# One more head transposed by VectorE in a two-layer masked attention kernel on one core: what the time does

## The chip, the core and the metric

The kernel runs on one core of a Trainium2 chip. The core has TensorE (PE in the profile; PEld is its weight load, which overlaps the matmuls), VectorE (DVE), ScalarE (ACT), GpSimd (POOL), SyncE (SP, which here only issues transfers) and 16 DMA engines that serve every transfer queue. The metric is device time in microseconds, the median of several executions.

## The reference

Two layers over 16 graphs of 1024 nodes with 256 features. Each normalises its input, clips it at zero, attends over the graph's adjacency matrix and adds the result to the input.

```
# layer 0: 8 heads of 32, masked by adj
h = maximum(layernorm(x), 0)
Q, K, V = heads of (h @ Wq.T + bq), (h @ Wk.T + bk), (h @ Wv.T + bv)
scores  = einsum('bhnd,bhmd->bhnm', Q, K) * 32 ** -0.5
attn    = softmax(where(adj == 0, -inf, scores))
x = x + (concatenated heads of attn @ V) @ Wo.T + bo
# layer 1: a score by kind of edge, with leaky relu
h = maximum(layernorm(x), 0)
e_k    = leaky_relu(einsum('bid,bjd->bij', h * a_k[:, 0], h), 0.2)     # k = 0..3
scores = where(adj == k + 1, e_k, -9e15)
x = x + softmax(scores) @ h
```

The adjacency holds 0 and 1 only, so the main path of layer 1 needs e_0 alone; a second path for other kinds stands behind a test at the end and does not run.

## The kernel before

A tile is 128 rows of one graph; a graph has NT = 8 tiles, the batch 128. One pass of the outer loop is called a slot here: slot s works on tile t = s mod 8 of graph s // 8 (`now`). Each slot has eight steps, h = 0 to 7, one for each head. The order of the instructions on every engine is the order in which this loop writes them (a manual schedule): nothing overtakes on an engine or on a queue. So a slot holds, interleaved by hand: layer 0 of tile s (`now`), the end of layer 0 of tile s-1 (`was`), the norm of tile s-2 (`gone`), layer 1 of tile s-9 (`edge`) and the end of layer 1 of tile s-10 (`edge_was`), and the projections of a tile that is wanted nine slots later (`piece`, `piece_was`). In the first nine slots there is no layer 1 yet; after the last slot a loop by itself ends the remaining tiles of layer 1 (the tail).

A head's way through layer 0:

- `scores(h)` (line 460): two matmuls of 512 columns into one of two PSUM places, `sides`. Heads 4 and 6 take the second, all others the first; layer 1's scores use the second too.
- `softmax_max(h)` (472): VectorE scales and masks the scores into an SBUF buffer p (ring of 4) and leaves the row extremum.
- `softmax_exp(h)` (489): ScalarE takes the exponential, one step later.
- The probabilities must be transposed. `turn` (589, 590) does it with eight 128x128 TensorE transposes into PSUM and two copies to SBUF. `turn_blocks` and `place_blocks` (381, 386) do it with one VectorE transpose inside 32x32 blocks into a buffer of the ring `blocks`, and four SyncE transfers of 128 KB that move the blocks to their places in a buffer pT (ring of 7). Which heads go which way is in `BY_BLOCKS` and `MIXED`: in tiles 1 to 6 heads 0, 1, 4, 5 by VectorE, in tile 0 heads 4, 5, in tile 7 heads 0, 1. Heads 6 and 7 always go by TensorE. It happens two steps after the scores: head 6 and head 7 of a tile in steps 0 and 1 of the next slot.
- A head whose rows are wanted in another order than the block transpose leaves them has its exponential written in permuted order into a second p buffer (`softmax_exp`, the branch on `MIXED`).
- `combine(0)` (525), 64 small matmuls in step 7, multiplies heads 0 to 3 by V; `combine(1)` does heads 4 to 7 in step 3 of the next slot. Its matmuls go round the heads: the first is of head 4, the second of head 5, the third of head 6, the fourth of head 7, and so on.

Of layer 1: `score` (625, 631), `softmax_max` (654), `bend` (663, a relu by ScalarE into its own buffer `less`), `leak` (672 to 674, GpSimd), `softmax_exp` (678), then `turn_blocks` and `place_blocks` in step 0 of the next slot, `gather` (696) in steps 5 and 6, `store` (703, 705) in step 6. `gather` sums into `sums_place`, which `combine` uses too.

SyncE's queue takes, in the order of the slot: layer 1's four pieces (step 0), head 0's four (step 2), head 1's four and the next queries (step 3), the output of layer 1 and head 4's four (step 6), the kept rows x1d (551, step 6), head 5's four (step 7), and in tiles 7 and 0 eight loads of keys between them.

The steps around the change, in the order of the code:

```
now.scores(h)
now.softmax_max(h)
ending.softmax_exp(eh)              # the head before
if h == 3: was.combine(1); piece_was.biased(); was.combined()
if turning and th in by_blocks(turning.t):
    turning.turn_blocks(th); turning.place_blocks(th)      # th = h - 2, of `was` in steps 0 and 1
if h == 0: edge.score(0); gone.normed(); edge_was.turn_blocks(); edge_was.place_blocks()
```

Of the kernel before, what the change touches and what calls it, by code (L numbers as in the profile page):

```python
# [8 lines left out]
F32 = mybir.dt.float32  # L9
# [5 lines left out]
ALU = mybir.AluOpType  # L15
AX = mybir.AxisListType

P = 128
HEADS = 8
HD = 32  # L20
# [4 lines left out]
NEG_INF = -9000000000000000.0  # L25
MASKED = -1e30
MIXED = (0, 1, 4, 5)
BY_BLOCKS = {7: (0, 1), 0: (4, 5)}


def by_blocks(t):
    return BY_BLOCKS.get(t, MIXED)

# [6 lines left out]
FLOOR = 1e28  # L40
# [7 lines left out]
def gnn_kernel(  # L48
# [35 lines left out]
    work = ctx.enter_context(tc.tile_pool(name="work", bufs=2))  # L84
# [103 lines left out]
    class Piece:  # L188
# [5 lines left out]
        def __init__(self, b, first, n=1):  # L194
            self.b, self.first, self.n = b, first, n
            self.cols = slice(first * P, (first + n) * P)
            self.projected, self.halved, self.queries = [], [], []
            self.tags = ("xin", "h0", "hT", "halves", "hTm") if n == 1 else ("pT", "pT", "pT", "p", "blocks")

        def buffer(self, i, shape, dtype=F32):  # L200
            tag = self.tags[i]
            if tag == "pT":
                return ptp.tile(shape, dtype, tag=tag, name=tag)
            bufs = {"p": 4, "blocks": 3, "halves": 2 if self.n == 1 else 4, "qt": 2, "xin": 2}.get(tag, 1)
            return work.tile(shape, dtype, tag=tag, name=tag, bufs=bufs)

        def load(self, queue=nc.gpsimd):
# [163 lines left out]
    def mixed(rows):  # L371

        return rows.rearrange("(b k) n -> k b n", b=NB)
# [3 lines left out]
        return rows.rearrange("(k b) n -> b k n", b=NB)  # L377

    def blocks_of(p):
        blocks = work.tile([P, NB, NT, HD], F32, tag="blocks", bufs=3)  # L380
        nc.vector.transpose(blocks.rearrange("p b j q -> p j b q"), p)  # L381
        return blocks.rearrange("p b j q -> p b (j q)")

# [8 lines left out]
    h1s, x1ds, masks = {}, {}, {}  # L392
# [22 lines left out]
    class Attend:  # L415
# [3 lines left out]
        def __init__(self, b, t):  # L419
            self.b, self.t = b, t  # L420
            self.rows = slice(t * P, (t + 1) * P)
            self.probs, self.turned = {}, {}

        def load_queries(self):
            self.qt = work.tile([P, HEADS, P], F32R, tag="qt")
            q = qds[self.b][self.t].rearrange("c (r d) u w n -> (d u w) (c r) n", d=HD)
            nc.sync.dma_start(out=self.qt.bitcast(F32), in_=q)
# [26 lines left out]
            )  # L454

        def scores(self, h):
            self.ps = sides[h in (4, 6)]
            for nh in range(N // HALF):
                cols = slice(nh * HALF, (nh + 1) * HALF)
                nc.tensor.matmul(  # L460
                    self.ps[:, cols],
                    lhsT=self.qt[:, h, :],
                    rhs=keysets[self.b][h][:, cols],
                    start=True,
                    stop=True,
                )

        def softmax_max(self, h):

            p = work.tile([P, N], F32, tag="p", bufs=4)  # L470
            nmx = small.tile([P, 1], F32, tag="nmx")
            nc.vector.tensor_tensor_reduce(  # L472
                out=p, in0=sides[h in (4, 6)], in1=self.neg, scale=-SCALE, scalar=FLOOR,
                op0=ALU.add, op1=ALU.min, accum_out=nmx,
            )
            self.probs[h] = (p, nmx)
# [20 lines left out]
        def turn_blocks(self, h):  # L497
            self.blocks = blocks_of(self.probs[h][0])
# [94 lines left out]
    class Edges:  # L593


        def __init__(self, b, t, last=False):
            self.b, self.t, self.last = b, t, last
            self.rows = slice(t * P, (t + 1) * P)
            self.side = sides[t % 2 if last else 1]
            self.tags = {"sel": ("p", 4), "pT1": ("pT", 7)} if last else {}  # L600
            if last and t % 2:
                self.tags |= {"ha": ("hT", 1), "x1b": ("x1", 1)}

        def buffer(self, tag, shape):
            tag, bufs = self.tags.get(tag, (tag, 1))
# [53 lines left out]
        def bend(self):  # L659

            if not self.last:
                self.less = work.tile([P, N], F32, tag="less", name="less", bufs=1)
                nc.scalar.activation(self.less, self.sel, AF.Relu, scale=1 - 1 / SLOPE)  # L663

        def leak(self):
# [20 lines left out]
        def turn_blocks(self):  # L686
            self.blocks = blocks_of(self.sel)
# [4 lines left out]
        def gather(self, half):  # L692

            for j in range(half * NT // 2, (half + 1) * NT // 2):
                for a in range(NB):
                    nc.tensor.matmul(  # L696
                        sums_place[a * HD : (a + 1) * HD, :], lhsT=self.pT[:, j, a], rhs=h1s[self.b][:, j, :],
                        start=(j == 0), stop=(j == NT - 1),
                    )

        def store(self):
            rec = small.tile([P, 1], F32, tag="rec1")
            nc.vector.reciprocal(rec, self.total)  # L703
            ot = work.tile([P, D], F32, tag="h0", bufs=1)
            nc.vector.scalar_tensor_tensor(ot, sums_place, rec, self.x1, ALU.mult, ALU.add)  # L705
            nc.sync.dma_start(out=mixed(out[self.b, self.rows, :]), in_=ot)


# [65 lines left out]
    def attend_of(s):  # L774
        return Attend(*divmod(s, NT)) if 0 <= s < B * NT else None
# [9 lines left out]
    with tc.manual_schedule():  # L785
        first = [Piece(0, 0, 4), Piece(0, 4, 4)]
        piece_was, piece_next = Piece(1, 0), piece_of(0)
        now, nxt = attend_of(0), attend_of(1)
# [39 lines left out]
        piece, edge, edge_was = piece_next, None, None  # L828
# [8 lines left out]
        for s in range(B * NT + 1):  # L837
            b, t = divmod(s, NT)
# [8 lines left out]
            for h in range(HEADS):  # L847
                ending, eh = (now, h - 1) if h >= 1 else (was, HEADS - 1)
                turning, th = (now, h - 2) if h >= 2 else (was, HEADS + h - 2)
# [38 lines left out]
                if h == 3:  # L888
                    if was:
                        was.combine(1)  # L890
                    if piece_was:
                        piece_was.biased()
                    if was:
                        was.combined()
                if turning and th in by_blocks(turning.t):
                    turning.turn_blocks(th)
                    turning.place_blocks(th)
                elif turning:
                    turning.turn(th, 0)
                    turning.turn(th, 1)  # L900


                if h == 0:
                    if edge:
                        edge.score(0)
                    if gone:
                        gone.normed()
                    if edge_was:
                        edge_was.turn_blocks()
                        edge_was.place_blocks()  # L910
                if h == 1:
                    if gone:
                        gone.turn_normed()
                    if piece_was:
                        piece_was.project(1, 0)
                        piece_was.project(1, 1)
                    if was:
                        was.reciprocals()
                    if piece_nxt:
                        piece_nxt.load()  # L920
                if h == 2:
# [54 lines left out]
            gone, was, now, nxt = was, now, nxt, nxt2  # L976
            edge_was, edge = edge, edge_nxt
# [85 lines left out]
```

## Time and profile before

| what | value |
|---|---|
| median of 3 runs | 3078.11 us (3077.22 to 3081.56) |
| the profiled execution's own time | 3080.43 us |
| its span in the trace | 3078.1 us |
| busy: PE, ACT, DVE, POOL | 2964.1, 2654.2, 2514.7, 2172.2 us |
| TensorE transposes of layer 0 (589) | 4608, busy 603.9 us |
| ScalarE copies of them (590) | 1024, mean 590 ns |
| VectorE block transposes of p (381) | 456, mean 1238 ns |
| transfers of block pieces (386) | 2304, median 3.4 us from issue to landing |
| granted TensorE clock, mean | 0.996 |

Busy time is the union of an engine's instructions. The mean of a TensorE matmul is longer than its share, because matmuls overlap: 4608 transposes of 274 ns each take 603.9 us together, 131 ns each. A wait is put down to the instruction or transfer that released it. The landing of a transfer is counted from its issue on the queue.

The profiled execution's time is 2.3 us over its span, for what lies around it, and 2.3 us over the median of the runs.

### The profile page before, as it was taken

How to read it: one execution, taken by the hardware profiler on the slowest of the kernel's cores; microseconds unless marked ns; L12 is line 12 of the kernel's file. 1: busy time of each engine (PE TensorE's matmuls, PEld its weight loads, DVE VectorE, ACT ScalarE, POOL GpSimd, SP SyncE). 2: the span in 40 equal slices, each digit the busy share in tenths (PEclk: the TensorE clock that was granted, in tenths of full speed). 3: DMA queues.
4: the chain of work that ended last, by engine and by line, in shares of the span. 5: the costliest groups of instructions: out<-in, count | busy, mean ns of one | idle time of the engine just before them, and what ended most of it. 6: DMA issues, size and time to landing. Idle time of an engine off the chain costs nothing. (4 is left out here: it accounts for less than half of the span.)

```text
span 3078.1 us, 96258 instructions
## 1 busy us (share of the span) xinstructions
PE 2964.1 (96%) x36722; PEld 2230.7 (72%) x36722; DVE 2514.7 (82%) x4453; ACT 2654.2 (86%) x5159; POOL 2172.2 (71%) x2999
## 2 busy tenths in 40 slices
PE   7889999999999999999999999999999999999997
PEld 4667777777777777777777777777777777776664
DVE  5878888888888888888888788888888888888884
ACT  5889888899888898889889888988989888898872
POOL 3657777777777777777777777777777777776542
PEclk9999999999999999999999999999999999999999
DMA  6776777878777786777777777787777777777653
GB/s 239 217 227 201 235 236 225 253 219 245 229 224 235 227 257 212 227 251 221 247 230 232 233 231 244 221 253 223 221 248 226 248 212 234 236 227 239 191 164 100
DMA packets 597828, 695.68 MB, mean 226 GB/s; under 512 B 63280, under 2 KB 528560, under 8 KB 597360
## 3 DMA queue, kind: packets, MB, share of 16 engines
q1 hardware_dynamic: 528288, 477.29, 52.0%
q0 software_dynamic: 66960, 210.04, 20.8%
q8 instruction: 295, 4.83, 0.7%
q10 hardware_dynamic: 2112, 2.10, 0.2%
q14 instruction: 173, 1.42, 0.1%
HBM read 252.98 MB, written 134.22 MB: 126 GB/s over the span
## 5 line engine op out<-in xcount | busy, mean ns | idle before, releaser
L472 DVE CUSTOM_DVE_ANT_0 p<-s,neg 128x1024 f32<-128x1024 f32 x1024 | 1235.6, 1207 | 220.8 <-PE s L460 189.5
L489 ACT ACTIVATE p<-p,nmx 128x1024 f32<-128x1024 f32 x1024 | 1249.6, 1224 | 135.5 <-DVE nmx L472 127.1
L460 PE MATMUL s<-k,qt 128*128 128x512 f32 x2048 | 759.3, 452 | 22.2 <-DVE nmx L472 13.8
L590 ACT COPY pT<-trp 128x512 f32<-128x512 f32 x1024 | 548.7, 590 | 92.8 <-PE trp L589 92.3
L589 PE MATMUL trp<-ident,p 128*128 128x128 f32 x4608 | 603.9, 274 | 3.6 <-ACT pT L590 1.5
L589 PEld LDWEIGHTS trp<-ident,p 128*128 128x128 f32 x4608 | 531.3, 140 | 101.7 <-DVE pT L590 9.6
L381 DVE STREAM_TRANSPOSE blocks<-p 128x1024 f32<-128x1024 f32 x456 | 564.4, 1238 | 12.7 <-ACT p L678 10.6
L525 PE MATMUL acc<-pT,v 128*32 128x128 f32 x16384 | 533.3, 275 | 36.9 <-ACT recT L519 24.9
L525 PEld LDWEIGHTS acc<-pT,v 128*32 128x32 f32 x16384 | 454.3, 110 | 146.3 <-ACT recT L519 79.9
L696 PE MATMUL acc<-h,pT 128*32 128x256 f32 x8192 | 493.0, 382 | 8.0 <-DVE ot L705 7.9
L440 POOL TENSOR_SCALAR neg<-adj 128x1024 bf16<-128x1024 int32 x128 | 467.7, 3654 | 43.7 <-ACT neg L452 34.4
L460 PEld LDWEIGHTS s<-k,qt 128*128 128x128 f32 x2048 | 322.0, 190 | 116.4 <-DVE nmx L472 43.7
L696 PEld LDWEIGHTS acc<-h,pT 128*32 128x32 f32 x8192 | 241.0, 109 | 210.3 <-issue 62.4
L674 POOL TENSOR_TENSOR sel<-sel,less 128x1024 f32<-128x1024 f32 x120 | 286.6, 2388 | 69.4 <-ACT less L663 48.1
L631 PE MATMUL s<-h1T,ha 128*128 128x512 f32 (+2 forms) x744 | 272.8, 490 | 2.6 <-ACT h1T L568 0.5
L672 POOL TENSOR_SCALAR less<-top 128x1 f32<-128x1 f32 x120 | 31.8, 265 | 272.9 <-DVE top L654 272.8
L324 POOL DMA_DIRECT2D qd<-halves x240 | 177.0, 777 | 58.7 <-POOL halves L314 31.8
L489 ACT ACTIVATION_READ_ACCUMULATOR p<-p,nmx 128x1 f32 x1024 | 206.8, 202 | 0.0
L509 POOL COPY wide<-rec 128x256 f32<-128x256 f32 x128 | 53.7, 419 | 208.9 <-DVE rec L507 208.9
L330 POOL DMA_DIRECT2D kd<-halves x240 | 171.7, 764 | 35.5 <-POOL halves L314 35.4
L314 POOL TENSOR_TENSOR halves<-full,halves 128x256 fp32r<-128x256 f32 x240 | 176.4, 735 | 20.6
L631 PEld LDWEIGHTS s<-h1T,ha 128*128 128x128 f32 x744 | 126.7, 190 | 70.7 <-issue 45.0
(117 smaller groups left out, 4323.1 us busy)
## 6 DMA issues: line engine op xcount, KB each, us to landing
pT<-blocks SPq DMA_DIRECT2D x2304, 128.0 KB, 3.4
qt<-qd SPq DMA_DIRECT2D x128, 512.0 KB, 4.6
k<-kd SPq DMA_DIRECT2D x128, 512.0 KB, 7.4
adj<-in_adj POOLq DMA_DIRECT2D x127, 512.0 KB, 4.9
qd<-halves POOLq DMA_DIRECT2D x240, 256.0 KB, 2.7
kd<-halves POOLq DMA_DIRECT2D x240, 128.0 KB, 4.0
xb<-in_x POOLq DMA_DIRECT2D x128, 128.0 KB, 4.1
x1d<-x SPq DMA_DIRECT2D x128, 128.0 KB, 3.8
```

What stands on the lines that cost most here:

```text
L324: nc.gpsimd.dma_start(out=qds[self.b][self.first, oc].rearrange("p u w n -> p u (w n)"), in_=halves.unsqueeze(1).to_broadcast([P, 2, 2 * P]),)
L381: nc.vector.transpose(blocks.rearrange("p b j q -> p j b q"), p)
L440: nc.gpsimd.tensor_scalar(self.neg, self.adj, 0.0, MASKED, ALU.is_equal, ALU.mult)
L460: nc.tensor.matmul(self.ps[:, cols], lhsT=self.qt[:, h, :], rhs=keysets[self.b][h][:, cols], start=True, stop=True,)
L472: nc.vector.tensor_tensor_reduce(out=p, in0=sides[h in (4, 6)], in1=self.neg, scale=-SCALE, scalar=FLOOR, op0=ALU.add, op1=ALU.min, accum_ ...
L489: nc.scalar.activation(to, of, AF.Exp, bias=nmx, scale=-1.0, accum_out=self.sums[:, h : h + 1])
L525: nc.tensor.matmul(sums_place[r * HD : (r + 1) * HD, g * P : (g + 1) * P], lhsT=vs[self.b][:, j, place_of(h) : place_of(h) + HD], rhs=self ...
L589: nc.tensor.transpose(tr[:, j, :], p[:, jj * P : (jj + 1) * P], ident)
L590: copy(pT[:, half * 4 : half * 4 + 4, :], tr)
L631: nc.tensor.matmul(self.side[:, cols], lhsT=self.ha[:, c, :], rhs=h1T[:, c, cols], start=(c == 0), stop=(c == NC - 1),)
L674: nc.gpsimd.tensor_tensor(self.sel, self.sel, self.less, ALU.subtract)
L696: nc.tensor.matmul(sums_place[a * HD : (a + 1) * HD, :], lhsT=self.pT[:, j, a], rhs=h1s[self.b][:, j, :], start=(j == 0), stop=(j == NT - 1),)
```

## The change

- `BY_BLOCKS`: head 6 goes by VectorE too in tiles 0 to 6 of every graph: 112 heads more. Tile 7 stays as it was. As head 6 is not in `MIXED`, its exponential is written in permuted order into a second p buffer.
- The ring `blocks` has four buffers instead of three, and layer 1's relu takes one of them instead of a buffer of its own.
- Layer 1's turn (its block transpose and four pieces) moves from step 0 to the end of step 1. Head 1's turn moves from step 3 to step 4, ahead of head 2's turn by TensorE.
- In the first nine slots the scores alternate between the two PSUM places head by head.
- In the tail, tiles with odd t gather into another PSUM place (`late`) and write their output through another buffer.

```diff
-BY_BLOCKS = {7: (0, 1), 0: (4, 5)}
+BY_BLOCKS = {7: (0, 1), 0: (4, 5, 6), 1: (0, 1, 4, 5, 6), 2: (0, 1, 4, 5, 6), 3: (0, 1, 4, 5, 6), 4: (0, 1, 4, 5, 6), 5: (0, 1, 4, 5, 6), 6: (0, 1, 4, 5, 6)}
...
-            bufs = {"p": 4, "blocks": 3, "halves": 2 if self.n == 1 else 4, "qt": 2, "xin": 2}.get(tag, 1)
+            bufs = {"p": 4, "blocks": 4, "halves": 2 if self.n == 1 else 4, "qt": 2, "xin": 2}.get(tag, 1)
...
-        blocks = work.tile([P, NB, NT, HD], F32, tag="blocks", bufs=3)
+        blocks = work.tile([P, NB, NT, HD], F32, tag="blocks", bufs=4)
...
+            self.second = (1, 3, 5, 7) if b * NT + t < LAG else (4, 6)
...
-            self.ps = sides[h in (4, 6)]
+            self.ps = sides[h in self.second]
...
-                self.tags |= {"ha": ("hT", 1), "x1b": ("x1", 1)}
+                self.tags |= {"ha": ("hT", 1), "x1b": ("x1", 1), "h0": ("xb", 1)}
+            self.sums = late if last and t % 2 else sums_place
...
-                self.less = work.tile([P, N], F32, tag="less", name="less", bufs=1)
+                self.less = work.tile([P, N], F32, tag="blocks", name="less", bufs=4)
...
-                        sums_place[a * HD : (a + 1) * HD, :], lhsT=self.pT[:, j, a], rhs=h1s[self.b][:, j, :],
+                        self.sums[a * HD : (a + 1) * HD, :], lhsT=self.pT[:, j, a], rhs=h1s[self.b][:, j, :],
...
-            ot = work.tile([P, D], F32, tag="h0", bufs=1)
-            nc.vector.scalar_tensor_tensor(ot, sums_place, rec, self.x1, ALU.mult, ALU.add)
+            ot = self.buffer("h0", [P, D])
+            nc.vector.scalar_tensor_tensor(ot, self.sums, rec, self.x1, ALU.mult, ALU.add)
...
+                if h == 4 and now and 1 in by_blocks(t):
+                    now.turn_blocks(1)
+                    now.place_blocks(1)
                 if turning and th in by_blocks(turning.t):
-                    turning.turn_blocks(th)
-                    turning.place_blocks(th)
+                    if h != 3:
+                        turning.turn_blocks(th)
+                        turning.place_blocks(th)
...
-                    if edge_was:
-                        edge_was.turn_blocks()
-                        edge_was.place_blocks()
                 if h == 1:
...
+                    if edge_was:
+                        edge_was.turn_blocks()
+                        edge_was.place_blocks()
```

More of the change, by code (lines that the diff above doesn't have):

```diff
@@ L472, in softmax_max @@
             nc.vector.tensor_tensor_reduce(
-                out=p, in0=sides[h in (4, 6)], in1=self.neg, scale=-SCALE, scalar=FLOOR,
+                out=p, in0=sides[h in self.second], in1=self.neg, scale=-SCALE, scalar=FLOOR,
                 op0=ALU.add, op1=ALU.min, accum_out=nmx,
```

## The prediction

> **What bounds the kernel now.** I read the page first (busy times), then busy time by stretch, then all waits, then one slot engine by engine, then the one place where TensorE had to wait long.
>
> ```profile
> PE 2964.1 (96%) x36722; PEld 2230.7 (72%) x36722; DVE 2514.7 (82%) x4453; ACT 2654.2 (86%) x5159; POOL 2172.2 (71%) x2999
> ```
> ```profile
> 500.00:2900.00 2400.00, 2364.25 (x29641) 1788.94 (x29640) 2009.43 (x3555) 2143.95 (x4175) 1782.80 (x2444) 1.00 0.76 232
> ```
>
> The second line is a stretch of 2400 us: busy PE, PEld, DVE, ACT, POOL, then granted clock and DMA share. TensorE is busy 98.5% of it at full clock, ACT 89%, DVE 84%. TensorE sets the pace, so its removed work is worth time, but only where no wait takes its place. What releases it is the question. One whole slot (67, tile 3; it starts at T0 = 1585.96 with head 0's scores and lasts 22.73 us):
>
> ```profile
> 1585.96 0.73 PE L460 MATMUL s<-k,qt 128*128 128x512 f32 x2
> 1586.53 1.04 PE L589 MATMUL trp<-ident,p 128*128 128x128 f32 x8
> 1587.40 0.38 PE L625 MATMUL s<-ident,mirror 128*128 128x128 f32 x2
> ...
> 1594.86 2.16 PE L525 MATMUL acc<-pT,v 128*32 128x128 f32 x64
> ```
> ```profile
> 1586.83 1.22 DVE L472 CUSTOM_DVE_ANT_0 p<-s,neg 128x1024 f32<-128x1024 f32 x1 [0.20 <-issue]
> 1587.98 0.08 DVE L472 DVE_READ_ACCUMULATOR2_ANT nmx<- 128x1 f32 x1
> 1587.98 1.24 DVE L381 STREAM_TRANSPOSE blocks<-sel 128x1024 f32<-128x1024 f32 x1
> ```
> ```profile
> 1587.69 13.67 SPq L386 DMA_DIRECT2D pT<-blocks  x16
> ...
> 1590.43 10.93 SPq L386 DMA_DIRECT2D pT<-blocks  x12
> ...
> 1594.06 7.30 SPq L386 DMA_DIRECT2D pT<-blocks  x8
> ```
>
> See four things. Head 6's eight transposes take 0.87 us of TensorE, start to next start. combine(1) starts 8.90 us after T0. On DVE, layer 1's block transpose stands right behind head 0's maximum and ends at T0+3.3. On SP (each line counts what is left of a run of issues) head 5's pieces go out from T0+1.7, layer 1's only when they are out, from T0+4.5 to T0+6.7, head 0's from T0+8.1.
>
> **The step that decides: head 6's pieces.** In the new order head 6's transpose stands on DVE exactly where layer 1's stood (behind head 0's maximum), and its pieces on SP exactly where layer 1's were (behind head 5's). So the trace has a stand-in for their landing. But layer 1's pieces were not wanted before gather in step 5, T0+14.7; head 6's are wanted by the third matmul of combine(1). I took, from the issue and landing times of all slots with layer 1, the landing of the fourth layer 1 piece and the start of combine(1), both from T0, means in us:
>
> | tile of the slot | slots | combine(1) starts | fourth piece lands (least to most) | sum of the lateness |
> |---|---|---|---|---|
> | 1 | 14 | 9.88 | 9.97 (9.27 to 10.52) | 2.7 |
> | 2 | 15 | 9.16 | 10.56 (9.55 to 12.57) | 21.1 |
> | 3 | 15 | 8.85 | 10.49 (9.82 to 11.39) | 24.6 |
> | 4 | 15 | 8.60 | 10.56 (9.73 to 11.66) | 29.4 |
> | 5 | 15 | 8.59 | 10.53 (9.18 to 12.39) | 29.0 |
> | 6 | 15 | 8.30 | 10.49 (9.71 to 12.30) | 32.8 |
> | 7 | 14 | 8.25 | 10.66 (9.86 to 11.52) | 33.6 |
>
> Tile 0's slot combines a tile 7, which is unchanged. Together 103 slots, 173 us, 1.68 each. The 0.87 us that TensorE no longer spends are already inside: they only make it arrive earlier at a wait that ends when it ends. From combine(1) to the next T0 TensorE works without a gap (13.83 us in most slots), so a late combine(1) delays the slot in full. The trace shows this where head 5's pieces came late by chance:
>
> ```profile
> PE acc L525 <- DMA pT<-blocks: 12.0, 15, 2.0
> ```
> ```profile
> 917.30 0.41 PE L525 MATMUL acc<-pT,v 128*32 128x128 f32 x2
> 919.73 3.50 PE L525 MATMUL acc<-pT,v 128*32 128x128 f32 x62 [2.02 <-DMA pT<-blocks]
> ```
> ```profile
> 917.00:920.00 3.00, 0.98 (x13) 0.44 (x15) 2.36 (x5) 2.33 (x4) 1.41 (x3) 0.99 0.88 267
> 920.00:922.00 2.00, 2.00 (x47) 2.00 (x42) 0.00 (x0) 1.50 (x4) 1.42 (x1) 0.50 0.81 240
> ```
>
> The first line (waiter, releaser; us, times, longest): 15 such waits. In slot 74 a piece was 1.30 late and the rest of the slot took 15.01 instead of 13.83. The other lines are slot 38: after two matmuls TensorE waits 2.02 us, and then **the granted clock is 0.50** for 3.41 us: the other 62 matmuls take 3.50 us instead of some 1.95, so this wait cost 3.84 in all, 1.6 more than itself.
>
> Bounds of the lateness: with the least landing of each row (mean 9.59 from T0, against 8.80 for combine(1)) 103 x 0.8 = 82 us; with the most (11.76) 103 x 3.0 = 305. I take 150, a little under the mean's 173: POOL's transfers, which fill the engines in that stretch, hang on layer 1's maximum, and combine(1)'s wait lets them run up to 1 us earlier in the slot. Against it: -14, the idle time that the trace already puts down to such pieces.
>
> The Trainium skill speaks here. "DMA: Bandwidth & Descriptors", section "Anatomy of one DMA — SWDGE (gpsimd) path", gives a fixed 2.0 us and bytes by 436 GB/s, an estimate of 2.3 us for a 128 KB piece (of a POOL-path transfer; these are SP's). The rows say median 3.4, least 2.4. By the page the fourth piece would land some 1 us earlier and two thirds of the 150 would be gone; I go by the rows.
>
> **The clock.** TensorE reaches combine(1) earlier than before: 0.87 less work, of which up to 0.5 goes to waiting for DVE, which has 1.24 more ahead of head 1's maximum (heads 1 to 3 share one PSUM place). So its idle stretch is the lateness plus 0.4 to 0.9, about 2.1 us in tiles 2 to 7 and under 1.2 in tile 1. The half clock comes in pieces of 3.41 us on a fixed grid; I summed the idle time of TensorE on that grid: a cell with 1.57 to 1.74 idle brought it three times and did not six times, 2.02 and 2.87 brought it, 1.4 and less never. With 1.7 as the limit an idle stretch of 2.1 lies so in a cell with chance (3.41 - 2.1 + 2 x 0.4) / 3.41 = 0.62: of 89 slots 55, at 1.62 each 89 us. Bounds: 0, and all 103 slots, 167.
>
> "TensorE: Matmul & The Clock Gate", section "Part 1: The HAM clock gate", lets the clock fall after an idle window of some 3.4 us; read as a whole window without work no wait here would do it and the 89 would be nothing. The 2.02 us row is against that.
>
> **The other parts.**
> - Removed: 112 x 8 transposes (the 0.87 above) and 112 x 2 ScalarE copies, 1.06 us a head. Added on ScalarE: the permuted exponential. Rows of tile 7's heads, which are permuted too: 2.25 us, plain 1.15. This head's stride is another that no row shows; lower bound no surcharge, upper twice the permuted row, 4.5. I take 2.25: net nothing. It is hidden, as it ends at T0-0.6 and is wanted at T0+2.0; uncovered 112 x 1.1 = 123.
>
> ```profile
> 1502.15 1.14 ACT L489 ACTIVATE p<-p,nmx 128x1024 f32<-128x1024 f32 x1
> 1505.23 2.25 ACT L489 ACTIVATE p<-p,nmx 128x1024 f32<-128x1024 f32 x1
> ```
> - DVE gets 112 x 1.24 = 139 us, 20.6 of a 24 us slot: hidden behind TensorE and the wait.
> - Four more SP issues (0.64 each). Behind them in the queue wait layer 1's pieces (landing near T0+13, wanted after T0+14.7) and head 0's (wanted in step 7): hidden.
> - Head 1's turn, now behind head 4's maximum: out some 5 to 7.7 us after combine(1), landed by 10.5, combine(0) wants it at 12. Hidden; a landing of 4.5 would still do. Ahead of it the queries are issued, 0.5 to 1.2 us. Before, these pieces had 3.1 us to spare on average.
> - Relu in the ring: it takes the buffer of head 5, whose pieces land at T0+8.2 on average; it starts at T0+9.2. Hidden; late by chance it would lie inside combine(1)'s wait.
> - First nine slots: alternating places can take away TensorE's waits on DVE's maxima, 5.2 us between 80 and 280 us. But head 6's chain is there too: from combine(1) to the next one, 2.2 for itself, some 13 of DVE (five maxima, five turns, the norm), 2 of issue, 3 to 4 of landing, about 21.6 to 22.6 against 21.3. -5 to +9, taken +4.
> - Tail: gather waits for the store 7.9 us in all; DVE's own chain (5.7 us a tile) stays. -8 to 0, taken -3.
>
> **Sum**, on the profiled execution's own 3080.4 us: 150 - 14 + 89 + 4 - 3 = +226, 3306.4; the median lies 2.3 under that execution, so 3304.
>
> **Rivals.**
> 1. The wait comes, the clock holds. For: a wait of 1.18 and one of 1.76 late kept the clock. Against: slot 38. 3304 - 89 = 3215.
> 2. Faster: head 6's pieces land in time. Place: combine(1); decides if the fourth lands by T0+8, 2.5 us earlier than the stand-in. That needs SP free when the transpose ends (T0+3.3) and four issues of 0.64 with the least landing of 2.4: T0+7.7. Against: SP is still at head 5's until T0+4.3 at best, and no stand-in landed before T0+9.18. It would give 0.4 to 0.87 on 103 slots, some 62 us: 3078 - 62 - 1 = 3015.
> 3. The lateness just equals what is saved, by pieces at T0+8.8: 3078. No row has it.
> 4. The DMA engines give out: 512 more packets a slot at 48 ns over 16 engines are 1.6 us on each, at a share of 0.76. If every landing slips by 1 us: 150 + 103, and the clock falls in nearly every slot, 160: some 3478.
>
> **How the numbers follow.** Forecast 0.58, rival 1 0.23, rival 2 0.08, rival 3 0.03, rival 4 0.08. Predicted 3304. The low end takes in rival 1 with 45 us less lateness, 3170; the high end 240 of lateness with the same clock, near 3400. By 0.2%, about 6 us, which is what runs of this kernel can tell: faster 0.08, the same 0.03, slower 0.89.
>
> **What would show it.** TensorE waiting at combine(1) for pieces in about 100 slots, near 200 us instead of 12; a mean granted clock near 0.97; TensorE's share near 89%; slots of 24 to 26 us; 3712 transposes; no wait at combine(0) or gather. Wrong if head 6's fourth piece lands before T0+8.5, if the added wait is on DVE or ACT, or if the permuted exponential is far from 2.25.

## The result, and the profile after

The changed kernel takes 3247.95 us, the median of four runs (3244.9 to 3257.52), against 3077.66 for the kernel before in four runs beside it: **slower, ratio 1.056 (95% interval 1.055 to 1.058)**. The prediction said 3304, with a range from 3170 to 3400. Its profiled execution took 3257.52 us, the slowest of the four, with a span of 3255.5, which is 177.4 more than the span before; all sums below are made against these two spans, while the medians differ by 170.3.

The page first: busy times, and the granted clock in 40 slices.

```profile
PE 2948.8 (91%) x35826; PEld 2171.6 (67%) x35826; DVE 2644.5 (81%) x4565; ACT 2642.9 (81%) x4935; POOL 2178.5 (67%) x2999
...
PEclk9899999999999999999999999999999999999999
```

TensorE has 896 instructions fewer, but is busy only 15 us less, and its share falls from 96% to 91%: what left it is idle time now, and more. The clock falls visibly in one slice only, the second, which is the first slots. Then the two stretches that the prediction reads (us; busy PE, PEld, DVE, ACT, POOL; granted clock; DMA share; GB/s):

```profile
80.00:280.00 200.00, 160.93 (x1748) 128.80 (x1750) 151.00 (x261) 155.39 (x299) 115.71 (x162) 0.91 0.71 213
500.00:2900.00 2400.00, 2214.03 (x27325) 1642.49 (x27324) 1998.96 (x3451) 2021.32 (x3793) 1706.42 (x2340) 0.99 0.79 239
```

In the body TensorE is idle 186 of 2400 us where it was idle 36; the clock stays at 0.99 there. In the first slots it is 0.91, against 0.97 before. What the idle time waits for (engine, line, releaser; us in all, times, longest):

```profile
ACT p L490 <- DVE blocks L381: 136.6, 112, 2.8
...
PE acc L526 <- DMA pT<-blocks: 134.1, 113, 3.0
...
PEld s L461 <- DVE nmx L473: 119.3, 145, 1.5
...
PE s L461 <- DVE nmx L473: 68.4, 88, 1.3
...
PEld acc L526 <- DMA pT<-blocks: 49.7, 37, 2.1
```

The second line is the wait of the forecast: 15 times and 12.0 us before, 113 times and 134.1 us now, of which 125.8 us are at combine(1) and 8.4 at combine(0). The third and fourth are more than the forecast had, which put up to 0.5 a slot at head 1's maximum alone. They are the scores that wait for the maximum of the head before, because both use one PSUM place; before they stood at 43.7 and 13.8 us. The first line is new too, 112 times, one for each changed head: the permuted exponential needs a second p buffer and waits for the block transpose that reads it. In slot 67 it starts 1.18 us late for that and ends at T0+0.64, where the prediction had T0-0.6; it is wanted at T0+2.06, so here the delay costs the transpose nothing.

The groups (line, engine, shapes, count | busy, mean ns | idle before, and its main releaser):

```profile
L461 PE MATMUL s<-k,qt 128*128 128x512 f32 x2048 | 753.6, 450 | 73.4 <-DVE nmx L473 68.4
L526 PE MATMUL acc<-pT,v 128*32 128x128 f32 x16384 | 594.4, 282 | 175.3 <-DMA pT<-blocks 134.1
...
L590 PE MATMUL trp<-ident,p 128*128 128x128 f32 x3712 | 489.1, 274 | 4.8 <-ACT pT L591 2.8
```

The transposes went from 603.9 to 489.1 us as meant. The idle time in front of `scores` and `combine` took more than that.

Slot 67 again, the slot that the prediction shows, in the changed kernel: T0 is 1676.60. First TensorE, then VectorE, then SyncE (start, us, engine, line, operation, idle before).

```profile
1676.60 0.73 PE L461 MATMUL s<-k,qt 128*128 128x512 f32 x2
...
1677.39 1.03 PE L633 MATMUL s<-h1T,ha 128*128 128x256 f32 x4
1678.80 0.74 PE L461 MATMUL s<-k,qt 128*128 128x512 f32 x2 [0.38 <-DVE nmx L473]
...
1685.27 0.59 PE L526 MATMUL acc<-pT,v 128*32 128x128 f32 x4
1687.03 1.94 PE L526 MATMUL acc<-pT,v 128*32 128x128 f32 x60 [1.17 <-DMA pT<-blocks]
```
```profile
1677.51 1.23 DVE L473 CUSTOM_DVE_ANT_0 p<-s,neg 128x1024 f32<-128x1024 f32 x1 [0.24 <-PE s L461]
...
1678.66 1.24 DVE L381 STREAM_TRANSPOSE blocks<-p 128x1024 f32<-128x1024 f32 x1
...
1681.32 1.25 DVE L381 STREAM_TRANSPOSE blocks<-sel 128x1024 f32<-128x1024 f32 x1
```
```profile
1678.25 0.59 SPq L552 DMA_DIRECT2D x1d<-x  x1
1678.95 11.12 SPq L386 DMA_DIRECT2D pT<-blocks  x16
```

See four things. Head 6's transpose (blocks<-p at T0+2.06) stands where layer 1's stood, and layer 1's (blocks<-sel) 2.66 us later. On SP the run of 16 issues is heads 5, 6, layer 1 and head 0, four each at 0.695 us: head 6's begin four issues after 1678.95, at T0+5.1, and the last goes out at T0+7.2. TensorE makes four matmuls of combine(1) from T0+8.67 and then stands until T0+10.4. And the second `scores` start at T0+2.20, after a wait of 0.38 for head 0's maximum, where head 6's transposes used to stand. In slot 70 that wait is 1.03:

```profile
1748.36 0.73 PE L461 MATMUL s<-k,qt 128*128 128x512 f32 x2
...
1750.56 0.73 PE L461 MATMUL s<-k,qt 128*128 128x512 f32 x2 [1.03 <-DVE nmx L473]
```

By tile of the slot, from the start and end times of the matmuls in slots 9 to 126, means in us (before → after; "idle" is the gap inside combine(1) after):

| tile | slots | combine(1) starts, from T0 | combine(1) ends, from T0 | idle | period of the slot |
|---|---|---|---|---|---|
| 0 | 14 | 9.51 → 9.58 | 11.47 → 11.54 | 0.00 | 24.33 → 24.40 |
| 1 | 15 | 9.88 → 9.15 | 12.06 → 12.53 | 0.84 | 23.57 → 24.14 |
| 2 | 15 | 9.16 → 8.71 | 11.41 → 12.58 | 1.23 | 23.05 → 24.22 |
| 3 | 15 | 8.85 → 8.69 | 11.04 → 12.39 | 1.15 | 22.69 → 24.04 |
| 4 | 15 | 8.60 → 8.68 | 10.95 → 12.58 | 1.27 | 22.59 → 24.28 |
| 5 | 15 | 8.59 → 8.68 | 10.90 → 12.47 | 1.15 | 22.53 → 24.11 |
| 6 | 15 | 8.30 → 8.69 | 10.82 → 12.58 | 1.25 | 22.46 → 24.23 |
| 7 | 14 | 8.25 → 8.68 | 10.74 → 12.90 | 1.35 | 24.06 → 26.72 |

The 177.4 us by stretch: slots 9 to 126 +160.0 (2730.9 → 2890.9), slots 1 to 8 +16.0 (171.8 → 187.8), all that lies ahead of slot 1 +1.3, the tail 0.1. Of the 160.0, 149.5 are there when combine(1) ends in tiles 1 to 7 (the differences of the means by their counts); of the other 10.5, 7.0 come later in tile 7's slots and 1.0 lies in tile 0's.

### The profile page after: what moved, and what is told of

The parts are those of the page before. It is cut to its first block, busy times and chain, and to the rows that moved or that the text cites. A ratio compares the mean times of both kernels' runs of the same rounds, so it can differ in the third digit from the quotient of the medians.

```text
span 3255.5 us, 95144 instructions
## 1 busy us (share of the span) xinstructions
PE 2948.8 (91%) x35826; PEld 2171.6 (67%) x35826; DVE 2644.5 (81%) x4565; ACT 2642.9 (81%) x4935; POOL 2178.5 (67%) x2999
## 5 line engine op out<-in xcount | busy, mean ns | idle before, releaser
L490 ACT ACTIVATE p<-p,nmx 128x1024 f32<-128x1024 f32 x1024 | 1363.4, 1336 | 244.1 <-DVE blocks L381 136.6
L526 PE MATMUL acc<-pT,v 128*32 128x128 f32 x16384 | 594.4, 282 | 175.3 <-DMA pT<-blocks 134.1
L381 DVE STREAM_TRANSPOSE blocks<-p 128x1024 f32<-128x1024 f32 x568 | 704.1, 1240 | 10.8 <-ACT p L680 10.7
L526 PEld LDWEIGHTS acc<-pT,v 128*32 128x32 f32 x16384 | 487.5, 113 | 312.8 <-issue 158.4
L591 ACT COPY pT<-trp 128x512 f32<-128x512 f32 x800 | 428.5, 588 | 133.8 <-PE trp L590 133.3
L590 PE MATMUL trp<-ident,p 128*128 128x128 f32 x3712 | 489.1, 274 | 4.8 <-ACT pT L591 2.8
L590 PEld LDWEIGHTS trp<-ident,p 128*128 128x128 f32 x3712 | 428.5, 141 | 88.6 <-ACT pT L591 10.8
L536 DVE TENSOR_TENSOR oT<-acc,recT 128x256 f32<-128x256 f32 x128 | 54.3, 424 | 220.3 <-ACT neg L453 134.8
L665 ACT ACTIVATE less<-sel 128x1024 f32<-128x1024 f32 x120 | 127.3, 1061 | 75.7 <-DVE top L656 72.9
```

Of the source, the lines that this page charges most:

```text
L490: nc.scalar.activation(to, of, AF.Exp, bias=nmx, scale=-1.0, accum_out=self.sums[:, h : h + 1])
L526: nc.tensor.matmul(sums_place[r * HD : (r + 1) * HD, g * P : (g + 1) * P], lhsT=vs[self.b][:, j, place_of(h) : place_of(h) + HD], rhs=self ...
L590: nc.tensor.transpose(tr[:, j, :], p[:, jj * P : (jj + 1) * P], ident)
L591: copy(pT[:, half * 4 : half * 4 + 4, :], tr)
```

## The experiments

Each kernel ran beside the kernel before on the same chip, whose median was 3073 to 3077 us; beside the changed kernel it was 3077.66, so a difference from the changed kernel is uncertain by up to 4.5 us. "Per slot" numbers are from each one's trace as in the table. Line numbers shift by one or two between kernels.

**1. Without head 6.** The other edits alone.

```diff
-BY_BLOCKS = {7: (0, 1), 0: (4, 5, 6), 1: (0, 1, 4, 5, 6), ...}
+BY_BLOCKS = {7: (0, 1), 0: (4, 5)}
```

> The changed kernel with head 6 given back to TensorE in all tiles; ring, moved turns, first slots and tail stay changed. Theory (head 6's pieces are the whole loss, the other edits are hidden): 3060 to 3082 us, no wait of some 130 us at combine(1) for pieces, clock halved only in the first slots. Rival (the moved turns or the shared ring cost something): over 3100 us.

Measured 3089.55, ratio 1.0044 (1.0027 to 1.006), 8 us over the range expected. So nearly all of the loss hangs on head 6, but the other edits are not free: +8.5 us in slots 9 to 126 and +6.5 in slots 1 to 8. In the body combine(1) starts 0.3 later in tiles 6 and 7 (8.60 and 8.54 against 8.30 and 8.25). In slots 1 to 6 combine(0) stands 11.3 us in all until head 1's pieces land, whose turn was moved back by a step; before the change it stood for nothing there. The half clock came there no more often than before.

**2. Head 6 alone.** The kernel before with the new `BY_BLOCKS` and nothing else.

```diff
-BY_BLOCKS = {7: (0, 1), 0: (4, 5)}
+BY_BLOCKS = {7: (0, 1), 0: (4, 5, 6), 1: (0, 1, 4, 5, 6), ...}
```

> The kernel before with head 6 by VectorE in tiles 0 to 6 and nothing else: three block buffers, relu in its own buffer, layer 1's turn behind head 6's in step 0, head 1's in step 3. Theory (the pieces set combine(1), the moves and the fourth buffer only keep DVE from coming late besides): no faster than the changed kernel, 3250 to 3330 us, as head 1's maximum comes 1.24 us later and a turn may wait for a block buffer. Rival (the moves themselves brought the loss): under 3200 us.

Measured 3423.39, ratio 1.112 (1.109 to 1.115), 93 us over the range expected. Its waits:

```profile
PEld s L460 <- DVE nmx L472: 395.5, 253, 4.5
PE s L460 <- DVE nmx L472: 321.1, 198, 4.3
...
DVE blocks L381 <- DMA pT<-blocks: 149.0, 99, 3.5
```

With three block buffers VectorE itself waits 99 times for a ring buffer whose pieces have not gone, and head 1's maximum stands behind that wait; TensorE's scores wait for the maximum, and combine(1) starts near T0+12. The clock went to half 53 times after slot 9. The fourth buffer and the moved turns are therefore worth 3423 - 3248 = 175 us *to head 6*, with the smaller edits among them, though by themselves all these cost 15.

**3. Head 6's pieces one place earlier in SP's queue.** The kept rows x1d go out behind them instead of ahead of head 5's.

```diff
+                    if gone:
+                        gone.keep()
...
-                    if was:
-                        was.keep()
...
+        gone.keep()
```

> The changed kernel with the transfer of the kept rows x1d moved on SP's queue from before head 5's pieces to behind head 6's. Theory (the place in SP's queue sets the landing): head 6's pieces go out 0.6 to 0.65 us earlier in some 104 slots, 65 us less, and with the shorter wait most of the ten later half-clock stretches go, 13 us: about 3170 us (3155 to 3200). Rival (the full DMA engines set the landing, not the queue): 3230 to 3250 us.

Measured 3205.76, ratio 1.0424 (1.0407 to 1.0442), 42 us less than with the whole change.

```profile
PE acc L526 <- DMA pT<-blocks: 97.0, 109, 2.0
```

That is 6 us over the range expected. Head 6's first issue comes at T0+4.33 instead of 5.13, its fourth piece lands at 10.01 instead of 10.39 (means), and combine(1) ends some 0.4 earlier (12.1 instead of 12.5). The direction is the queue's; of 0.80 at the issue 0.38 arrive at the landing, so the landing follows the issue in part only. What takes the rest was not tested.

**4. Work of TensorE moved in front of the wait.** Head 2's eight transposes ahead of combine(1) instead of behind it.

```diff
+                    if now:
+                        now.turn(2, 0)
+                        now.turn(2, 1)
...
-                elif turning:
+                elif turning and not (h == 4 and th == 2):
```

> The changed kernel with head 2's TensorE transposes moved ahead of combine(1), so that 0.87 us of work lies in the wait. Theory (TensorE stands idle some 1.2 us at combine(1) and nothing else is short there): combine(1) ends when it did, what follows has 0.87 less, of which some 0.3 comes back as a wait of the output projection for VectorE: 104 x 0.57 = 59 us and 13 us of half clock less, about 3176 us (3150 to 3195). Rival (the wait only shows up there, VectorE sets the slot): 3235 to 3250 us.

Measured 3185.53, ratio 1.0379 (1.0344 to 1.0415), as expected. combine(1) starts at 9.49 instead of 8.68 and its idle time falls from 1.2 to 0.65; the rest of the slot is 0.5 to 0.6 shorter. Work of 0.87 us put into the wait is work that is no longer on the path.

**5. Both 3 and 4.**

> The kept rows behind head 6's pieces and head 2's transposes ahead of combine(1), both in one. Theory (one wait of 1.25 us, which the two shorten by 0.6 and 0.87): the wait is gone in most slots, slots of 22.6 to 22.9 us, 3070 to 3110 us: the change's saving does not appear even then, as TensorE waits for head 0's maximum where head 6's transposes stood. Rival (the transposes were worth 0.87 us a slot and the wait alone hid it): under 3020 us.

Measured 3155.19, ratio 1.0266 (1.0249 to 1.0283): missed. The two give 93 us together against 42 and 62 singly; the idle time at combine(1) is down to 0.05 to 0.59, but TensorE's transposes now wait 37.1 us for ScalarE's exponential (30.5 in experiment 4, 0.8 in the changed kernel). There was a next wait close behind.

**6. Both, and the query projection into step 0.** It fills the wait for head 0's maximum.

```diff
+                    if piece_was:
+                        piece_was.project(1, 0)
+                        piece_was.project(1, 1)
...
-                    if piece_was:
-                        piece_was.project(1, 0)
-                        piece_was.project(1, 1)
```

> As e5_both, and the query projection (0.81 us of TensorE) moved from step 1 to step 0, ahead of layer 1's scores, into the stretch in which TensorE waits for head 0's maximum. Theory (that stretch is short of work in tiles 4 to 7 only, and head 1's maximum comes later in the others): 10 to 40 us under e5_both. Rival (VectorE's chain from head 0's to head 2's maximum sets combine(1)): within 10 us of it, or over.

Measured 3200.42, ratio 1.0408 (1.0389 to 1.0426): 45 us worse than 5, where my theory had it better. Both places of the projection lie ahead of combine(1), so the same work only changed places, and combine(1) starts later for it: 11.34, 10.36 and 10.13 in tiles 1 to 3 instead of 9.95, 9.49 and 9.47. The place that it left costs more than the one that it fills saves. The theory that TensorE's gaps can simply be filled fell; the rival, that VectorE's chain of maxima sets the pace there, fits.

**7. Eight transposes that nobody reads, where head 6's were.** TensorE gets back the amount of work that the change removed.

```diff
+                if h == 0 and turning and th in by_blocks(turning.t):
+                    for _ in range(2):
+                        idle = ps_tr.tile([P, 4, P], F32, tag="tr", name="idle")
+                        for j in range(4):
+                            nc.tensor.transpose(idle[:, j, :], ident, ident)
```

> The changed kernel with eight transposes of the identity, which nobody reads, where head 6's eight stood in step 0: the removed TensorE work is given back, the pieces stay. Theory (those 0.87 us lay beside head 0's maximum and then inside the wait for the pieces): no more than 15 us from the changed kernel either way, 3233 to 3263 us, rather lower as the clock halves less often. Rival (TensorE's work counts in every slot): 112 x 0.87 = 97 us more, 3345 us.

Measured 3240.01, ratio 1.0533 (1.0513 to 1.0553): 896 transposes *more*, and 8 us *less*, or 3.5 less if each is counted from the kernel before that ran beside it (166.8 over it against 170.3). In tiles 4 to 7 combine(1) starts at 8.68 to 8.70 with the transposes and at 8.68 to 8.69 without them. The work that was removed is worth nothing that can be measured in this order.

**8. The first nine slots with the scores in the old places.**

```diff
-            self.second = (1, 3, 5, 7) if b * NT + t < LAG else (4, 6)
+            self.second = (4, 6)
```

> The changed kernel with the first nine slots' scores in one place as before. Theory (alternating only lets TensorE arrive earlier at combine(1) and wait longer, with the clock halved in nearly each of these slots): the stretch from slot 1 to slot 9 takes 178 to 188 us against 187.8, the whole within 10 us of the changed kernel, fewer than 11 half-clock stretches before slot 9. Rival (alternating takes off the 5 us that it could): 5 to 10 us more.

Measured 3231.59, ratio 1.0519 (1.0496 to 1.0541), 16 us less. That is 6 us more of a gain than the theory allowed. Slots 1 to 8 take 183.6 instead of 187.8, and the half clock comes there three times, as before the change, instead of ten times. They still take 11.8 us more than before the change: combine(0) stands 7.7 us in them for head 1's pieces. The span of slots 9 to 126 also came out shorter, 2872.9 instead of 2890.9, though nothing in them differs, in the one profiled execution of each. So the alternation is a loss in this kernel, but its 16 us don't all show where it acts. Of the 18 us in slots 9 to 126 some 10 are clock, by an estimate: 5 half-clock pieces instead of 11, at 1.62 each.

**9. Nobody waits for head 6's pieces.** The same instructions and transfers, but combine(1) takes its probabilities elsewhere.

```diff
-                        rhs=self.turned[h][:, j],
+                        rhs=self.turned[7 if h == 6 and 6 in by_blocks(self.t) else h][:, j],
```

> The changed kernel, but where head 6 went by VectorE combine(1) multiplies head 7's probabilities in its place: head 6's contribution is left out of the result, its turn and its four pieces are still made and still travel, only nobody waits for them. Theory (the wait for the pieces is the whole loss beside the first slots, and the removed transposes alone bring next to nothing): combine(1) runs without a gap, slots 9 to 127 take 2715 to 2745 us against 2731 before, the whole 3065 to 3095 us. Rival 1 (the removed transposes are worth 0.87 us a slot): 2990 us. Rival 2 (the load on the DMA engines and on VectorE costs by itself): over 3130 us.

Measured 3117.26, ratio 1.0133 (1.0104 to 1.0163), between the theory's range and rival 2's. So some 130 of the 170 us are this one wait, with the half clock behind it (one piece in slots 9 to 126 instead of 11). Two more things show. Without it combine(1) ends at 10.9 in tiles 3 to 7, where it ended at 10.7 to 11.0 *before* the change, with 0.87 us more work ahead of it. And the kernel is still slower than before: the rest of the slot is 12.0 to 12.24 in tiles 2 to 6 instead of 11.64. Its waits:

```profile
PEld s L461 <- DVE nmx L473: 120.8, 146, 1.6
...
PE s L461 <- DVE nmx L473: 68.2, 87, 1.3
...
PE acc L526 <- DMA pT<-blocks: 34.7, 38, 2.7
```
```profile
1583.64 0.41 PE L526 MATMUL acc<-pT,v 128*32 128x128 f32 x2
1585.03 1.95 PE L526 MATMUL acc<-pT,v 128*32 128x128 f32 x62 [0.99 <-DMA pT<-blocks]
```

The waits for head 0's maximum stand as they are in the changed kernel. The 34.7 us are now mostly at combine(0), as in the second fence (one slot's combine(0)): after two matmuls it waits for pieces. Head 1's, whose turn the change put off by a step, land after combine(0) has started in 37 of 104 slots; before the change they never did.

**10 to 12. Another head.** If the place of head 6 is the trouble, a head whose pieces have more time should cost less. Head 2's are only wanted in step 7. Kernel 10 is the kernel before with head 2 by VectorE in all tiles, the reciprocals' transposes a little earlier, and the query load on GpSimd's queue:

```diff
-BY_BLOCKS = {7: (0, 1), 0: (4, 5)}
+BY_BLOCKS = {7: (0, 1, 2), 0: (2, 4, 5), **{t: (0, 1, 2, 4, 5) for t in range(1, 7)}}
...
-            nc.sync.dma_start(out=self.qt.bitcast(F32), in_=q)
+            (nc.gpsimd if self.b + self.t else nc.sync).dma_start(out=self.qt.bitcast(F32), in_=q)
```

> The kernel before, with head 2 instead of head 6 by VectorE (all tiles), where its transposes stand in step 4 and its pieces are wanted in step 7; the reciprocals' transposes ahead of layer 1's second scores, their copy ahead of head 2's longer exponential, the queries loaded from GpSimd's queue so that SP is free for the pieces. Theory (a transpose is worth its 0.87 us only where TensorE has no wait beside it, and there VectorE's chain from combine(1) to the next head 0 is 12.4 us against TensorE's 11.6, so that VectorE sets the slot): within 1.5% of before, 3040 to 3120 us. Rival 1 (TensorE sets it): 128 x 0.87 us less, some 2975 us. Rival 2 (pieces again late at combine(0)): over 3150 us, with the wait in step 7.

Measured 3099.99, ratio 1.0084 (1.0065 to 1.0104): only 23 us lost, with sixteen heads more moved than by the change. It splits by tile: tile 0's slots fall from 24.33 to 22.65, all others grow by 0.07 to 0.73.

Kernel 11 adds head 1's turn ahead of the product oT in step 3.

```diff
+                    if turning and 1 in by_blocks(turning.t):
+                        turning.turn_blocks(1)
+                        turning.place_blocks(1)
```

> As e10_head2, with head 1's block transpose ahead of the product with the reciprocals in step 3, so that VectorE works on it while TensorE is in combine(1). Theory (VectorE's chain sets the slot): 0.5 us a slot or some 50 us under e10_head2, and its pieces go out 1 us earlier. Rival (TensorE waits for the product instead): the same or over.

Measured 3084.9, ratio 1.0031 (1.002 to 1.0043): 15 us better, not the 50 expected.

Kernel 12 keeps what paid: head 2 by VectorE in tile 0 only, where VectorE turns two heads instead of four, with the earlier reciprocals in that slot alone.

```diff
-BY_BLOCKS = {7: (0, 1), 0: (4, 5)}
+BY_BLOCKS = {7: (0, 1), 0: (2, 4, 5)}
...
+            (nc.gpsimd if self.t == 1 else nc.sync).dma_start(out=self.qt.bitcast(F32), in_=q)
...
+                if h == 3 and was and now and t == 0:
+                    was.turned_reciprocals()
...
+                    if was and now and t == 0:
+                        was.turn_reciprocals()
```

> The kernel before with head 2 by VectorE in tile 0 alone (and in its slot the reciprocals' transposes and copy earlier, the queries from GpSimd's queue); all other slots as before. Theory (an added block transpose pays only in a slot in which ScalarE is the late one and whose pieces are wanted late: in e10_head2 and e11_head2_turn1 the slots of tile 0 went from 24.33 to 22.65 and 22.73 us, all other slots got longer): 16 x 1.6 = 25 us less than before, 3045 to 3060 us. Rival (tile 0's slots were shorter only because the slots around them were late): within 6 us of before.

Measured **3048.97 us, ratio 0.990 (0.989 to 0.992)**: it beats the kernel before by 28 us and the changed one by 199. Its busy times:

```profile
PE 2943.9 (97%) x36594; PEld 2214.0 (73%) x36594; DVE 2532.3 (83%) x4469; ACT 2647.8 (87%) x5127; POOL 2186.7 (72%) x3015
```

Only 128 transposes are gone, and TensorE's share *rises* from 96% to 97%. Tile 0's slots fall from 24.33 to 22.82, 1.5 us in each of 16; the others keep their length within 0.2. But only half of the 1.5 can be the removed transposes, which stood behind combine(1): the time from its end to the next slot falls by 0.72 (12.86 to 12.14). The other 0.79 is there when combine(1) ends (11.47 to 10.68), and it is the moved reciprocals. Before, combine(1) waited in tile 0's slots 0.75 on average for their copy, as in slot 64; with kernel 12 it waits 0.03.

```profile
1524.28 1.95 PE L525 MATMUL acc<-pT,v 128*32 128x128 f32 x64 [0.69 <-ACT recT L519]
```

No run moved the reciprocals or the queries alone, so the split rests on these places in the slot.

## Why the prediction was right, and where its terms were not

The direction, the place and the first mechanism, the wait at combine(1) for head 6's pieces, were right, and the time lay in the range. The second mechanism, the clock that falls behind that wait, mostly did not come: it was 89 of the sum's +226, where the profiled executions show +177.4. By its steps:

| term | predicted | measured | how measured |
|---|---|---|---|
| lateness at combine(1), less the waits that were there | 150 - 14 = 136 | 133 | 149.5 at combine(1)'s end, less the 16 of the clock |
| clock in slots 9 to 126 | 89 | 16 | 11 half-clock pieces in these slots, 1 before the change, x 1.62 |
| first nine slots | +4 | +16.0 | slots 1 to 8; ahead of them +1.3 |
| tail | -3 | 0.1 | from slot 127's T0 to the end |
| all that was "hidden" | 0 | 10.5 | after combine(1)'s end, 7.0 of it in tile 7's slots, and 1.0 in tile 0's |

Of its signs, the mean granted clock came out at 0.986 and not near 0.97, TensorE's share at 91% and not near 89%, and combine(0), which was to wait for nothing, waited 8.4 us in all.

**The stand-in was right.** The prediction took layer 1's pieces of before as a measure for head 6's, since they have the same place behind the same neighbours: 10.47 from T0, the mean over its table. Head 6's fourth piece landed at 10.39 (8.43 to 11.55). Experiment 9 shows that this wait is what costs, experiment 3 that its length follows the place in SP's queue in part, experiment 4 that the wait can be filled. That 136 and 133 lie so close is partly luck. Measured as the prediction measured it (landing of the fourth piece against the start of combine(1) before), the lateness is 165 us, not 150: the pieces came only 0.08 earlier than the stand-in, so POOL's transfers gave back little. Part of what brings it down again is that combine(1) ends 2.08 after the landing, where it takes 2.18 in all when nothing holds it up: its first matmuls are already done. The rule of the Trainium skill that the prediction weighed against it ("DMA: Bandwidth & Descriptors", "Anatomy of one DMA — SWDGE (gpsimd) path": an estimate of 2.3 us for a piece), which the page gives for the POOL path, would have been too short for SP's pieces: they took 3.3 us in the median.

**The step that failed is the idle stretch, "about 2.1 us in tiles 2 to 7", and with it the clock.** It held that TensorE comes to combine(1) earlier by 0.87 less at most 0.5. It came at 8.75 on average, against 8.81: hardly earlier at all. The 0.87 us had stood beside head 0's maximum, for which the next scores wait; without the transposes the scores wait by themselves, slot 70 for 1.03. The prediction had priced that wait for head 1's maximum, behind the new transpose, and not for head 0's, where the transposes were taken out. In tiles 6 and 7 it even came 0.4 later than before, of which 0.3 are there in experiment 1, without head 6's move. The four matmuls that combine(1) makes before it stands (0.59 in slot 67) are not idle time either. So the idle stretch is 0.84 to 1.35, not 2.1. The limit of 1.7 that it read from the grid held well: in slots 1 to 126 of both kernels, grid pieces with 1.87 or more idle always brought the half clock, some between 1.57 and 1.80 did, and none with less, but for one of 1.09 that ran at half clock itself. 55 falls were forecast in those slots and 10 more than before came; the 73 us are more than the whole miss of 49.

This also says what the removed transposes were worth: nothing in the change (experiment 7 puts as many back and is no slower). Where nobody waits for the pieces (experiment 9), combine(1) ends earlier by 0.75, 0.36 and 0.12 in tiles 1 to 3, not at all in 4 and 5, and later by 0.10 and 0.18 in 6 and 7: 15 us by the counts of the slots, of 104 x 0.87 = 90. The prediction never needed the 90, but rival 2 did: with the pieces in time it would have brought 15 and not "some 62".

**The first nine slots** were outside their bounds of -5 to +9, and the larger part of it is the clock, in the one place where it does fall often. With alternating PSUM places the scores no longer wait, TensorE comes to combine(1) at 7.48 instead of 8.25, and finds head 6's pieces missing:

```profile
119.45 0.71 PE L461 MATMUL s<-k,qt 128*128 128x512 f32 x2
121.42 0.59 PE L526 MATMUL acc<-pT,v 128*32 128x128 f32 x4 [1.25 <-ACT recT L520]
122.79 3.50 PE L526 MATMUL acc<-pT,v 128*32 128x128 f32 x60 [0.78 <-DMA pT<-blocks]
```
```profile
119.40:122.80 3.40, 1.36 (x10) 0.65 (x11) 2.99 (x6) 3.25 (x8) 1.42 (x3) 0.97 0.71 186
122.80:126.20 3.40, 3.40 (x60) 3.15 (x60) 0.00 (x0) 0.84 (x2) 3.40 (x1) 0.53 0.77 205
```

Neither wait is long, 1.25 and 0.78, but the first and most of the second lie in one piece of the grid. The window of the fence is busy 1.36 of 3.40; the grid's own piece, 119.19 to 122.60, is idle for 1.92 of 3.41, and the next one runs at half clock (0.53 in the fence's window, which reaches a little beyond it). Slots 1 to 8 have 10 such pieces instead of 3: 7 x 1.62 = 11.3 of the 16.0. Another 4.2 us are combine(0)'s waits for head 1's pieces, in slots 1, 4, 5 and 6, a cost that the prediction held to be hidden. The prediction summed DVE's chain there and left its own rule for the clock out. Experiment 8 takes the alternation away and gains 16 us, 4.2 of them seen in these slots.

**"Hidden" edits.** ScalarE's permuted exponential took 2.20 us in the median (2.08 to 2.24) where 2.25 was taken; it ended at T0+0.63 on average, not at T0-0.6, and was still in time. DVE is busy 130 us more. Layer 1's pieces are hardly waited for at gather (3.3 us of idle time there in all). Head 1's turn was hidden thinly: its pieces had 3.14 us to spare before combine(0) on average and now 1.58, as forecast; but some come late (combine(0) stands 0.22 in tile 7's slots on average, and 4.2 us in the first nine), and experiment 9 shows them as the next wait. Experiment 1 prices all edits but head 6 at 15 us together, where the prediction had +1, first slots and tail.

**The rivals.** 1 (no clock fall, 3215) was nearer than the forecast, 33 us off against 56, and nearer in what happens from slot 9 on; what it lacks are the first slots, the falls that there were after slot 9, and the later waits. 2 and 3 fall with the landing times. 4 falls too: the packets of the four pieces (576 a changed slot by the pages' counts, where 512 were taken) raised the DMA share from 0.76 to 0.79, and a piece took 3.3 us in the median, not longer than the 3.4 before.

**What stays open.** In experiment 9 some 40 us over the kernel before remain: the rest of the slot is 0.3 to 0.6 longer in tiles 1 to 6 and 0.9 in tile 7's. From combine(0)'s start on it is 0.27 of 0.46 in tiles 2 to 6 and 0.89 of 0.93 in tile 7's, with combine(0)'s own idle time at 0.08 to 0.23 and 0.59. What the part ahead of combine(0) waits for was not separated; ScalarE's wait for the block transposes (134.2 us there) is one candidate that no run took away. The miss of experiment 5 was only named by its next wait, not tested. That experiment 8 came out 18 us shorter in slots that it does not touch was seen in one trace, and why the clock fell less often there no run looked into. How much of kernel 12's gain is the moved reciprocals was read from places in the slot and not tested by a run of its own.

## What to carry to other kernels

Work taken from the busiest engine is worth only what doesn't lie beside another wait: find the instruction that comes next and ask what it would wait for if the work were gone. A moved transfer is priced best by a transfer that has the same neighbours in the same queue before, and its landing is compared with the moment at which it is wanted, slot by slot. Where a step has many copies, change it in the copies in which the engine that takes the work has room: head 2 in all tiles cost 23 us, in tile 0 alone it gained 28, nearly half of it through the reciprocals that were moved with it. An edit that comes along with a change has to be priced by itself.

## What the runs showed of the hardware that was not expected

- The half clock needs no single long wait: gaps of 1.25 and 0.59 and a rest of 0.07, 1.9 us idle together in one 3.41 us piece of the grid, brought it, and stretches of 1.2 us seldom did. The Trainium skill ("TensorE: Matmul & The Clock Gate", "Part 1: The HAM clock gate") has the clock fall after an idle window of some 3.4 us; these rows show it with the window 44% busy.
- The permuted exponential costs ScalarE 2.20 us in the median for 128x1024 with head 6's stride and 2.25 to 2.27 with that of tile 7's heads 4 and 5, against 1.15 in plain order: in these two cases the two orders differ by 3% at most.
- 448 more transfers of 128 KB (2752 against 2304) left the median landing as it was (3.3 us against 3.4). Sixteen of them in a row took 11.12 us to go out, 0.695 each, and head 6's stood behind four others; taking one issue away from in front of them brought the landing 0.38 earlier.
